# The last four tiles finished by VectorE alone, and an order of instructions searched at build

## The chip, the cores and the metric

The kernel runs on one NeuronCore of a Trainium2 chip. The metric is the device time of one execution in microseconds. It is given as the median of three runs. The core has a matrix engine (TensorE, PE in the profile, with its weight loads as PEld), three engines for elementwise work (VectorE or DVE, ScalarE or ACT, GpSimd or POOL), and SyncE (SP), whose queue issues nearly all the DMAs here.

## The reference

The input x has 4 rows of 1024 tokens with 512 features; each row has a condition vector of 256 numbers, which is used twice.

```python
hidden  = concatenate([cond, cond], axis=-1)                 # (4, 512)
x_mean  = mean(x, axis=1)                                    # (4, 1, 512)
fused   = concatenate([x, x_mean * ones, hidden * ones], -1) # (4, 1024, 1536)
out     = x + relu(einsum('bld,do->blo', fused, W) + b)      # W is (1536, 512)
```

The mean and the condition are the same for all tokens of a row. So the kernel computes, per row, one bias vector of 512 numbers from them, and multiplies only x with the first 512 rows of W. Everything is fp32.

## The kernel before, in words

The output is cut into 32 tiles of 128 tokens by 512 features, eight to a row. A tile is accumulated in one PSUM bank; five banks serve the tiles in turn (`O_BANKS`). [...] 

The stages around them are these.

- x comes in twice. For row 0 it is transposed on TensorE (`turn`, L299, pieces 0 to 9). For rows 1 to 3 it comes in again as `z`, in blocks of 32 tokens, and VectorE transposes it (L301, pieces 10 to 33). A piece is one slice `j` of a unit of one to four tiles.
- ScalarE rounds each piece to its high part and sums it over the tokens (`hi`, L318). VectorE, or POOL for some pieces of rows 1 and 2, subtracts to get the low part (`lo`, L334).
- Row r's sums go into `total`, and VectorE adds four products of W with them to an accumulator in PSUM (`term`, L396). The accumulator is split in two (`acc_hi`, `acc_lo`), and TensorE multiplies both with a constant matrix so that the bias stands in all 128 partitions (`bias_product`, L421). ScalarE copies it to SBUF (`bias`, L427).
- A finished tile goes through four steps. VectorE adds the bias while it moves the tile from PSUM to SBUF (`freed`, L505), which also frees the PSUM bank. ScalarE applies relu (L510), POOL adds x (`finished`, L513), and SP stores the tile (L525). The first four tiles are moved by ScalarE (L502) before the bias is there, and POOL adds it later. Tile 30 gets relu and x in one VectorE instruction (L518). Tile 31 is computed in two halves of 256 features. Each half gets the bias on TensorE, by two more matmuls (L484), and relu and x by L518.

The order of instructions on each engine is made at build by the class `Plan`. Each step is added with a key, the engines that can do it with a cost in microseconds, the keys that it depends on, a due time, and a function that emits it. Going backwards from the due times, `latest_starts` gives each step its latest start. `run` then repeatedly takes, among the steps that could start first on an engine, the one with the earliest latest start. `NEVER` is a due time that presses on nothing. The engines then execute their lists in order, waiting on semaphores. SP's queue keeps its order too: a store that waits for its tile holds the stores and loads behind it.

Of the kernel before, what the change touches and what calls it, by code (L numbers as in the profile page):

```python
# [1 line left out]

# [10 lines left out]
ALU = mybir.AluOpType  # L13
# [5 lines left out]
class Plan:  # L19
# [5 lines left out]


    HANDOVER = 0.2
    PATIENCE = 0.1

    def __init__(self, engines):  # L30
# [29 lines left out]
                        ready.append(d)  # L60
        return start

    def run(self):
        latest = self.latest_starts()
        assert len(latest) == len(self.todo)
        while self.todo:
            could = []
            for key, (costs, deps, _, _, _) in self.todo.items():
                if not all(d in self.done for d in deps):
                    continue  # L70
                options = []
                for engine, cost in costs.items():
                    start = self.free[engine]
                    for d in deps:
                        end, later, by = self.done[d]
                        if by != engine:
                            end += later + self.HANDOVER
                        start = max(start, end)
                    options.append((start + cost, start, engine, cost))
                _, start, engine, cost = min(options)  # L80
                could.append((start, latest[key], key, engine, cost))
            assert could, list(self.todo.items())[:8]
            first = min(could, key=lambda t: t[:2])
            start, _, key, engine, cost = min(
                (t for t in could if t[3] == first[3] and t[0] <= first[0] + self.PATIENCE),
                key=lambda t: (t[1], t[0]),
            )
            _, _, _, emit, later = self.todo.pop(key)
            self.log.append((start, engine, key, start - self.free[engine]))
            self.free[engine] = start + cost  # L90
            self.done[key] = (start + cost, later, engine)
            emit(engine)


@with_exitstack
def kernel(
# [23 lines left out]
    B, L, D = x.shape  # L120
# [14 lines left out]
    FIRST = 7.3  # L135
    NEVER = 1000.0
    TURN_PE = (0, 1, 2, 3)
    SINGLY = 2
    KEEP = 4
    LO_POOL = {(r, u, j) for r in (1, 2) for u in (0, 1) for j in (1, 3)}  # L140
# [113 lines left out]
    for n, u in enumerate(by_z):  # L254
        for i in range(NQ):
            deps = [("turn", c) for c in range(len(pieces)) if n >= Z_BUFS and pieces[c][0] == by_z[n - Z_BUFS]]
            plan.add(("z", u, i), {"sp": SPZ}, deps, NEVER,
                     lambda e, u=u, i=i: load_z(u, i), later=3.0)
    x_order = ["w", 0, 1, "cond"] + list(range(2, B * NK // G))
    for n, g in list(enumerate(x_order))[4:]:  # L260
        was = x_order[n - X_BUFS]
        deps = ([("w_lo", j) for j in range(J)] if was == "w" else
                [("add_cond", k) for k in range(KH)] if was == "cond" else
                [("finished", was * G + i) for i in range(G)])
        plan.add(("x", g), {"sp": 4 * SP}, deps, NEVER,
                 lambda e, g=g: load_x(g), later=3.0)

# [70 lines left out]
    for c, (u, js) in enumerate(pieces):  # L338
        r, k0, n = units[u]
        deps = ([x_here(t) for t in range(last_tile[u] - n + 1, last_tile[u] + 1)]  # L340
                if u in TURN_PE else [("z", u, i) for i in range(NQ)])
        if c:
            deps.append(("turn", c - 1))
        same = [v for v in range(c) if (v in by_pool) == (c in by_pool)]
        if len(same) >= 2:
            deps.append(("lo", same[-2]))
            if len(pieces[same[-2]][1]) > 1:
                deps.append(("sum", same[-2]))
        if r == 1 and c == first_piece[1]:
            deps.append(("term", 0, KH + J - 1))  # L350
        w = n * len(js)
        plan.add(("turn", c), {"pe": 0.12 * w} if u in TURN_PE else {"dve": 0.14 + 0.24 * w}, deps,
                 FIRST + 1.3 * c - 1.0 if u in TURN_PE else NEVER,
                 lambda e, c=c: turn(c))
        deps = [("turn", c)]
        if c >= S_BUFS:
            v, js_v = pieces[c - S_BUFS]
            deps += made(last_tile[v], js_v[-1])
        plan.add(("hi", c), {"act": 0.16 + 0.2 * (len(js) == 1) + 0.108 * w}, deps, NEVER,
                 lambda e, c=c: split_hi(c))  # L360
        plan.add(("lo", c), {"pool": 1.33} if c in by_pool else {"dve": 0.15 + 0.135 * w},
                 [("hi", c)], NEVER, lambda e, c=c: split_lo(e, c))
        if len(js) > 1:
            plan.add(("sum", c), {"dve": 0.65}, [("lo", c)], NEVER, lambda e, c=c: add_up(c))
# [105 lines left out]
    def product(t, j, h=None, parts=(0, 1, 2)):  # L470
        r, k = divmod(t, NK)
        u = unit_of[r, k]
        p = piece_of[u, j]
        c = pieces[p][1].index(j) * units[u][2] + k - units[u][1]
        c = slice(c * P, (c + 1) * P)
        key = t if h is None else (t, h)
        d = slice(0, D) if h is None else slice(h * D // 2, (h + 1) * D // 2)
        w = d.stop - d.start
        if key not in pos:
            todo[key] = 3 * J  # L480
            pos[key] = ps_o.tile([P, D], F32, tag="po", name=f"po{t}_{h}")
            if h is not None:
                for n, v in enumerate((acc_hi[r], acc_lo[r])):
                    nc.tensor.matmul(  # L484
                        pos[key][:, :w], lhsT=mean, rhs=v[:, d], start=(n == 0), stop=False
                    )
        for n in parts:
            v, m = ((hi, w_hi), (hi, w_lo), (lo, w_hi))[n]
            nc.tensor.matmul(  # L489
                pos[key][:, :w], lhsT=v[p][:, c], rhs=m[:, j, d],  # L490
                start=(h is None and todo[key] == 3 * J),
                stop=(todo[key] == 1),
            )
            todo[key] -= 1
# [6 lines left out]
    def keep(t):  # L501
        nc.scalar.activation(o_tile(t), pos[t], AF.Copy)  # L502

    def add_bias(e, t):
        nc_of[e].tensor_tensor(  # L505
            o_tile(t), outs[t] if t < KEEP else pos[t], biases[t // NK], ALU.add
        )

    def relu(t):
# [4 lines left out]

    def relu_add_x(t, h=None):
        d = slice(0, D) if h is None else slice(h * D // 2, (h + 1) * D // 2)
        v = outs[t] if h is None else pos[t, h][:, : D // 2]
        nc.vector.scalar_tensor_tensor(  # L518
            o_tile(t)[:, d], v, 0.0, x_tile(t)[:, d], ALU.max, ALU.add
        )  # L520
# [6 lines left out]
    for t in range(NT):  # L527
        r, k = divmod(t, NK)
        u = unit_of[r, k]
        for h in (0, 1) if t == LAST else (None,):  # L530
# [3 lines left out]
                free.append(("freed", t - O_BANKS))  # L534
            if h == 1:
                free.append(("freed", t + 1 - O_BANKS))
            if h == 0:
                free.append(("acc_lo", r))
            for j in range(J):
                c = piece_of[u, j]  # L540
# [15 lines left out]
                plan.add(("product", key, j), {"pe": 0.7 if h is None else 0.36},  # L556
                         deps, FIRST + 2.8 * t + (0.7 if h is None else 0.36) * (j + 1) + 1.4 * (h or 0), lambda e, t=t, j=j, h=h: product(t, j, h))
        room = [("stored", t - O_BUFS)] if t >= O_BUFS else []
        if t == LAST:
            for h in (0, 1):  # L560
                deps = [("product", (t, h) if h else t, J - 1), x_here(t)] + ([] if h else room)
                plan.add(("finish", t, h), {"dve": 0.42}, deps, NEVER, lambda e, t=t, h=h: relu_add_x(t, h))
                plan.add(("stored", t, h), {"sp": SP}, [("finish", t, h)], FIRST + 2.8 * t + 8,
                         lambda e, t=t, h=h: store(t, h), later=2.0)
            continue
        whole = made(t, J - 1)
        if t < KEEP:
            plan.add(("freed", t), {"act": 0.6}, whole, NEVER, lambda e, t=t: keep(t))
            plan.add(("added", t), {"pool": 1.33}, [("freed", t), ("bias", r)], NEVER, lambda e, t=t: add_bias(e, t))
            plan.add(("relu", t), {"act": 0.63}, [("added", t)], NEVER, lambda e, t=t: relu(t))  # L570
            biased = ("relu", t)
        else:
            plan.add(("freed", t), {"dve": 0.7}, whole + [("bias", r)] + room, NEVER,
                     lambda e, t=t: add_bias(e, t))
            biased = ("freed", t)
            if t < NT - 2:
                plan.add(("relu", t), {"act": 0.63}, [("freed", t)], NEVER, lambda e, t=t: relu(t))
                biased = ("relu", t)
        if t < NT - 2:
            plan.add(("finished", t), {"pool": 1.33}, [biased, x_here(t)], NEVER,  # L580
                     lambda e, t=t: add_x(t))
        else:
            plan.add(("finished", t), {"dve": 0.74}, [biased, x_here(t)], NEVER,
                     lambda e, t=t: relu_add_x(t))
        plan.add(("stored", t), {"sp": SP}, [("finished", t)], min(FIRST + 2.8 * (t + 9), FIRST + 2.8 * NT + 3), lambda e, t=t: store(t), later=2.0)

    plan.run()
    return plan
# [27 lines left out]
```

## Time and profile before

| what | value |
|---|---|
| median of 3 runs | 109.43 us (109.39 to 109.77) |
| the profiled execution, its own time | 110.05 us |
| span in its profile | 108.3 us |
| TensorE clock granted | 0.989 over the span |
| TensorE busy | 102.4 us, 95% |
| VectorE, ScalarE, POOL busy | 78.2, 56.0, 67.4 us |
| DMA moved | 26.31 MB |

The profile is of one execution, and the span runs from its first to its last instruction. The profiled execution took 1.8 us more than its span. Busy shares are averages over the whole span. Which engine sets the time is read from the chain that ended last: it goes back from the last instruction, at each step to what released it. Matmuls are pipelined, so a matmul row lasts about 0.40 us while the next one starts 0.23 us later; starts tell more than lengths.

### The profile page before, as it was taken

The page shows a single profiled execution, that of the slowest core. Times are in us where ns is not written, and L with a number is a line of the kernel's source. Part 1 is how long each engine was busy: PE and PEld are TensorE (multiplying, and loading weights), DVE is VectorE, ACT ScalarE, POOL GpSimd, SP SyncE. Part 2 cuts the span into 40 slices and gives each one's busy share as a digit, 9 for nine tenths or more (in the row PEclk, how much of TensorE's full clock was granted, in tenths as well). Part 3 has the DMA queues.
Part 4 walks back from the last instruction along what each step waited for, and adds up shares of the span by engine and source line. Part 5 has one row for each costly group of instructions (what it writes and reads, how often), then busy time and mean ns, then how long its engine had stood idle before and what let it go on. Part 6 is the DMA issues. An engine that isn't in the chain of part 4 may idle for free.

```text
span 108.3 us, 1476 instructions
## 1 busy us (share of the span) xinstructions
PE 102.4 (95%) x455; PEld 81.0 (75%) x455; DVE 78.2 (72%) x115; ACT 56.0 (52%) x126; POOL 67.4 (62%) x61
## 2 busy tenths in 40 slices
PE   5999999999999999999999999999999999999930
PEld 2466888887888878777887878878788787887920
DVE  1048932559999999839999999499999990462830
ACT  5047376798778794149657243295356040392000
POOL 5000009849999999999899996029640840099800
PEclk9999999999999999999999999999999999999995
DMA  3699999999999999999999999999983222015364
GB/s 92 180 368 397 379 432 203 197 201 200 202 203 193 265 208 227 282 250 279 332 398 355 286 338 285 259 400 403 397 322 123 97 97 97 0 41 223 124 232 156
DMA packets 22945, 26.31 MB, mean 243 GB/s; under 512 B 1173, under 2 KB 13721, under 8 KB 22810
## 3 DMA queue, kind: packets, MB, share of 16 engines
q1 hardware_dynamic: 22928, 26.22, 86.3%
q8 instruction: 3, 0.05, 0.2%
q14 instruction: 4, 0.03, 0.1%
q10 hardware_dynamic: 10, 0.01, 0.0%
HBM read 17.83 MB, written 8.39 MB: 242 GB/s over the span
## 4 chain that ended last, share of the span: by engine, by line
PE 94%; DVE 1%; ACT 1%; issue 0%
PE po_None L489 80%; PE xT L299 4%; PE pw L175 4%; PE po L489 3%; PE pb L421 2%; PE pw L308 1%; ACT hi L318 1%; PE po L484 0%; DVE o L518 0%; DVE warm L166 0%; PE pt L377 0%; DVE ones L168 0%
## 5 line engine op out<-in xcount | busy, mean ns | idle before, releaser
L489 PE MATMUL po_None<-w_hi,hi 128*128 128x512 f32 x124 | 49.7, 401 | 0.2 <-ACT hi L318 0.2
L513 POOL TENSOR_TENSOR o<-o,x 128x512 f32<-128x512 f32 x30 | 38.1, 1300 | 18.0 <-ACT o L510 16.1
L489 PE MATMUL po_None<-w_hi,lo 128*128 128x512 f32 x124 | 49.1, 397 | 0.0
L489 PE MATMUL po_None<-w_lo,hi 128*128 128x512 f32 x124 | 48.6, 396 | 0.0
L318 ACT ACTIVATE hi<-xT 128x512 fp32r<-128x512 f32 (+1 forms) x34 | 19.7, 579 | 20.7 <-DVE xT L301 11.4
L489 PEld LDWEIGHTS po_None<-w_hi,hi 128*128 128x128 f32 x124 | 23.4, 189 | 6.3 <-ACT hi L318 0.7
L489 PEld LDWEIGHTS po_None<-w_hi,lo 128*128 128x128 f32 x124 | 23.3, 188 | 5.5
L489 PEld LDWEIGHTS po_None<-w_lo,hi 128*128 128x128 f32 x124 | 23.3, 188 | 5.3
L301 DVE STREAM_TRANSPOSE xT<-z 128x512 f32<-128x512 f32 x24 | 25.5, 1102 | 0.2
L505 DVE TENSOR_TENSOR o<-po_None,bias 128x512 f32<-128x512 f32 x27 | 17.4, 684 | 11.2 <-issue 4.4
L334 DVE TENSOR_TENSOR lo<-xT,hi 128x512 fp32r<-128x512 f32 (+1 forms) x26 | 16.4, 640 | 11.9 <-ACT hi L318 11.7
L510 ACT ACTIVATE o<-o 128x512 f32<-128x512 f32 x30 | 17.9, 627 | 4.5 <-POOL o L505 2.4
L396 DVE SCALAR_TENSOR_TENSOR acc<-w_mean,tot,acc 128x512 f32<-128x512 f32 x16 | 12.1, 756 | 0.6
L385 POOL TENSOR_TENSOR wc<-w_cond 128x512 f32<-128x512 f32 x2 | 2.5, 1288 | 14.0 <-DMA w_cond<-in_L_cond_W_dram 14.0
L334 POOL TENSOR_TENSOR lo<-xT,hi 128x512 fp32r<-128x512 f32 x8 | 10.5, 1317 | 0.4 <-ACT hi L318 0.4
L427 ACT ACTIVATE bias<-pb 128x512 f32<-128x512 f32 x4 | 2.4, 599 | 11.3 <-PE pb L421 11.3
L299 PEld LDWEIGHTS xT<-ident,x 128*128 128x128 f32 x32 | 5.7, 206 | 1.3 <-issue 0.5
L318 ACT ACTIVATION_READ_ACCUMULATOR hi<-xT 128x1 f32 x32 | 6.2, 193 | 0.0
L407 POOL TENSOR_TENSOR cond<-cond,term 128x512 f32<-128x512 f32 x4 | 5.2, 1300 | 1.4 <-ACT term L402 1.2
L299 PE MATMUL xT<-ident,x 128*128 128x128 f32 x32 | 5.8, 298 | 0.0
L402 ACT ACTIVATE term<-wc,cT 128x512 f32<-128x512 f32 x8 | 5.5, 720 | 0.3 <-POOL cond L407 0.3
L407 POOL TENSOR_TENSOR cond<-bL,term 128x512 f32<-128x512 f32 x4 | 5.2, 1296 | 0.7 <-ACT term L402 0.7
(47 smaller groups left out, 54.6 us busy)
## 6 DMA issues: line engine op xcount, KB each, us to landing
out_dram<-o SPq DMA_DIRECT2D x31, 256.0 KB, 6.7
x<-in_x_dram SPq DMA_DIRECT2D x7, 1024.0 KB, 9.6
z<-in_x_dram SPq DMA_DIRECT2D x24, 256.0 KB, 9.7
w_x<-in_L_cond_W_dram SPq DMA_DIRECT2D x4, 256.0 KB, 6.0
w_cond<-in_L_cond_W_dram SPq DMA_DIRECT2D x1, 1024.0 KB, 9.8
w_mean<-in_L_cond_W_dram SPq DMA_DIRECT2D x1, 1024.0 KB
x<-in_x_dram SPq DMA_DIRECT2D x2, 256.0 KB, 3.6
x<-in_x_dram SPq DMA_DIRECT2D x1, 512.0 KB, 7.1
```

Source lines behind the costliest of these rows:

```text
L175: nc.tensor.matmul(pw, lhsT=warm[:, :P], rhs=warm, start=True, stop=True)
L299: nc.tensor.transpose(v[:, (m * n + i) * P : (m * n + i + 1) * P], x_t[:, j], ident)
L301: nc.vector.transpose(v[:, : n * P].rearrange("p (n t) -> p n t", t=Q), zs[u].rearrange("p n (a j) -> p n j a", j=J)[:, : n * NQ, js[0], :],)
L318: nc.scalar.activation(hi[c][:, :m], xT[c][:, :m], AF.Copy, accum_out=sums[:, r, js[0], s : s + 1] if len(js) == 1 else None,)
L334: nc_of[e].tensor_tensor(lo[c][:, :m], xT[c][:, :m], hi[c][:, :m].bitcast(F32), ALU.subtract)
L396: nc.vector.scalar_tensor_tensor(acc[r], w_mean[:, j, :], totals[r][:, j : j + 1], acc[r], ALU.mult, ALU.add)
L402: nc.scalar.activation(terms[r, k], wc[:, k], AF.Copy, scale=cT[:, k, r : r + 1])
L407: nc.gpsimd.tensor_tensor(conds[r], conds[r] if k else bL, terms[r, k], ALU.add)
L489: nc.tensor.matmul(pos[key][:, :w], lhsT=v[p][:, c], rhs=m[:, j, d], start=(h is None and todo[key] == 3 * J), stop=(todo[key] == 1),)
L505: nc_of[e].tensor_tensor(o_tile(t), outs[t] if t < KEEP else pos[t], biases[t // NK], ALU.add)
L510: nc.scalar.activation(outs[t], outs[t], AF.Relu)
L513: nc.gpsimd.tensor_tensor(outs[t], outs[t], x_tile(t), ALU.add)
```

## The change

The change has four parts.

1. The last four tiles (`ALONE = 28`) take neither ScalarE nor POOL. VectorE adds the bias in place in PSUM (`biased`), and a second VectorE instruction applies relu, adds x and writes the tile to SBUF. The left half of tile 31 gets its bias in this way too; the right half keeps the two bias matmuls.
2. The order is no longer the first that the rule gives. `simulate` runs the rule without emitting anything. `run` does this 1500 times, with some of the latest starts shifted by random amounts (a fixed seed), and keeps the order with the smallest sum of two simulated ends: the plain one, and one in which every engine but TensorE is 3% slower (`slower_end`).
3. New dependencies keep the order of buffers that rotate: z loads one after another, x loads one after another, `hi` and `freed` in order of pieces and tiles.
4. Due times of stores change: for a tile t, the smaller of its old rule and a fixed time near the end, and `NEVER` for the last four.

```diff
+    TRIES = 1500
+    SLOWER = 1.03
...
+        for n in range(self.TRIES):
+            trial = dict(shifts)
+            if best:
+                for key in luck.sample(list(latest), 1 + n % 12):
+                    trial[key] = luck.gauss(0.0, 3.0)
+            found = self.simulate({k: v + trial.get(k, 0.0) for k, v in latest.items()})
+            found = (found[1] + self.slower_end(found[0]),) + found
+            if not best or found[0] <= best[0]:
+                best, shifts = found, trial
+        _, self.log, _, self.free = best
+        for _, engine, key, _ in self.log:
+            self.todo[key][3](engine)
...
+    ALONE = 28
...
+            if n or i:
+                deps.append(("z", u, i - 1) if i else ("z", by_z[n - 1], NQ - 1))
...
+        if n > 4:
+            deps.append(("x", x_order[n - 1]))
...
-        deps = [("turn", c)]
+        deps = [("turn", c)] + ([("hi", c - 1)] if c else [])
...
-            if h is not None:
+            if h:
                 for n, v in enumerate((acc_hi[r], acc_lo[r])):
                     nc.tensor.matmul(
                         pos[key][:, :w], lhsT=mean, rhs=v[:, d], start=(n == 0), stop=False
...
+    def add_bias(e, t, h=None):
+        d = slice(0, D) if h is None else slice(h * D // 2, (h + 1) * D // 2)
+        v = outs[t] if t < KEEP else pos[t if h is None else (t, h)][:, : d.stop - d.start]
         nc_of[e].tensor_tensor(
+            v if t >= ALONE else o_tile(t), v, biases[t // NK][:, d], ALU.add
         )
...
-        v = outs[t] if h is None else pos[t, h][:, : D // 2]
+        v = pos[t] if h is None else pos[t, h][:, : D // 2]
...
+        if t:
+            room.append(("freed", t - 1))
+        due = min(FIRST + 2.8 * (t + 9), FIRST + 2.8 * NT - 8)
+        if t >= ALONE:
+            for h in (0, 1) if t == LAST else (None,):
+                key = (t, h) if h else t
+                cost = 0.7 if h is None else 0.42
+                ready = [("product", key, J - 1)]
+                if not h:
+                    plan.add(("biased", t), {"dve": cost}, ready + [("bias", r)], NEVER, lambda e, t=t, h=h: add_bias(e, t, h))
+                    ready = [("biased", t)] + room
+                plan.add(("freed", key), {"dve": cost}, ready + [x_here(t)], FIRST + 2.8 * (t + 1) + 1.5 + (h or 0),
+                         lambda e, t=t, h=h: relu_add_x(t, h))
+                plan.add(("stored", key), {"sp": SP}, [("freed", key)], NEVER,
                          lambda e, t=t, h=h: store(t, h), later=2.0)
             continue
```

The order that comes out differs from the old one as follows. SP's last stores were those of tiles 27, 30, 28, 29, 31 left, 31 right; they are now 24, 28, 25, 27, 29, 26, 30, 31 left, 31 right. POOL's last addition was tile 29; it is now tile 26, after 24, 25 and 27. The bias product of row 1 stood after the second slice of tile 12 and now stands before its first; that of row 2 stood after the first slice of tile 20 and now stands before the last slice of tile 19; that of row 3 stays after the first slice of tile 28. In the head TensorE takes the same single matmuls and transposes in another order. The x load of tiles 8 to 11 is issued in the middle of the `z` loads of unit 6 instead of after them, and that of tiles 16 to 19 after the store of tile 11 instead of before that of tile 8.

More of the change, by code (lines that the diff above doesn't have):

```diff
@@ L1 @@
+import random
 from contextlib import ExitStack
@@ L61, in latest_starts, with simulate @@
         return start
[L63 to L66, printed above, removed]
-            could = []
[L68 to L80, printed above, removed]
+    def simulate(self, latest):
+        free, done = dict(self.free), dict(self.done)
+        missing, followers, ready = {}, {}, []
+        for key, (_, deps, _, _, _) in self.todo.items():
+            open_deps = {d for d in deps if d not in done}
+            missing[key] = len(open_deps)
+            for d in open_deps:
+                followers.setdefault(d, []).append(key)
+            if not open_deps:
+                ready.append(key)
+        since = {}
+        log = []
+        while ready:
+            could = []
+            for key in ready:
+                costs, deps, _, _, _ = self.todo[key]
+                if key not in since:
+                    since[key] = {
+                        engine: max([0.0] + [
+                            end + (later + self.HANDOVER if by != engine else 0.0)
+                            for end, later, by in (done[d] for d in deps)
+                        ]) for engine in costs
+                    }
+                _, start, engine, cost = min(
+                    (max(free[e], since[key][e]) + c, max(free[e], since[key][e]), e, c)
+                    for e, c in costs.items()
+                )
                 could.append((start, latest[key], key, engine, cost))
-            assert could, list(self.todo.items())[:8]
             first = min(could, key=lambda t: t[:2])
@@ L87, in run, with slower_end @@
             )
[L88 to L92, printed above, removed]
+            ready.remove(key)
+            log.append((start, engine, key, start - free[engine]))
+            free[engine] = start + cost
+            done[key] = (start + cost, self.todo[key][4], engine)
+            for f in followers.get(key, ()):
+                missing[f] -= 1
+                if not missing[f]:
+                    ready.append(f)
+        assert len(log) == len(self.todo)
+        return log, max(free.values()), free
+    def slower_end(self, log):
+        free, done = dict(self.free), dict(self.done)
+        for _, engine, key, _ in log:
+            costs, deps, _, _, later = self.todo[key]
+            start = max([free[engine]] + [
+                end + (wait + self.HANDOVER if by != engine else 0.0)
+                for end, wait, by in (done[d] for d in deps)
+            ])
+            free[engine] = start + costs[engine] * (1.0 if engine == "pe" else self.SLOWER)
+            done[key] = (free[engine], later, engine)
+        return max(free.values())
+    def run(self):
+        latest = self.latest_starts()
+        luck = random.Random(1)
+        best, shifts = None, {}
+        for n in range(self.TRIES):
[10 more added lines that the diff above has]
+            self.todo[key][3](engine)
 @with_exitstack
@@ L490, in product @@
                 pos[key][:, :w], lhsT=v[p][:, c], rhs=m[:, j, d],
-                start=(h is None and todo[key] == 3 * J),
+                start=(not h and todo[key] == 3 * J),
                 stop=(todo[key] == 1),
@@ L502, in keep @@
         nc.scalar.activation(o_tile(t), pos[t], AF.Copy)
-    def add_bias(e, t):
+    def add_bias(e, t, h=None):
+        d = slice(0, D) if h is None else slice(h * D // 2, (h + 1) * D // 2)
+        v = outs[t] if t < KEEP else pos[t if h is None else (t, h)][:, : d.stop - d.start]
         nc_of[e].tensor_tensor(
-            o_tile(t), outs[t] if t < KEEP else pos[t], biases[t // NK], ALU.add
+            v if t >= ALONE else o_tile(t), v, biases[t // NK][:, d], ALU.add
         )
@@ L536 @@
                 free.append(("freed", t + 1 - O_BANKS))
-            if h == 0:
+            if h:
                 free.append(("acc_lo", r))
@@ L558 @@
         room = [("stored", t - O_BUFS)] if t >= O_BUFS else []
[L559 to L563, printed above, removed]
+        if t:
[12 more added lines that the diff above has]
+                plan.add(("stored", key), {"sp": SP}, [("freed", key)], NEVER,
                          lambda e, t=t, h=h: store(t, h), later=2.0)
             continue
-        whole = made(t, J - 1)
+        whole = made(t, J - 1) + ([("freed", t - 1)] if t else [])
         if t < KEEP:
@@ L569 @@
             plan.add(("added", t), {"pool": 1.33}, [("freed", t), ("bias", r)], NEVER, lambda e, t=t: add_bias(e, t))
-            plan.add(("relu", t), {"act": 0.63}, [("added", t)], NEVER, lambda e, t=t: relu(t))
-            biased = ("relu", t)
+            biased = ("added", t)
         else:
@@ L575 @@
             biased = ("freed", t)
[L576 to L585, printed above, removed]
+        plan.add(("relu", t), {"act": 0.63}, [biased], NEVER, lambda e, t=t: relu(t))
+        plan.add(("finished", t), {"pool": 1.33}, [("relu", t), x_here(t)], NEVER, lambda e, t=t: add_x(t))
+        plan.add(("stored", t), {"sp": SP}, [("finished", t)], due, lambda e, t=t: store(t), later=2.0)
     plan.run()
```

## The prediction

> **What bounds the kernel now.** I read the page first (busy shares), then the chain that ended last in order of time, then the timelines of VectorE (DVE), GpSimd (POOL) and SyncE (SP) over the last microseconds, then the DMA landings of two short windows. The page says which engine is full:
>
> ```profile
> span 108.3 us, 1476 instructions
> PE 102.4 (95%) x455; PEld 81.0 (75%) x455; DVE 78.2 (72%) x115; ACT 56.0 (52%) x126; POOL 67.4 (62%) x61
> PEclk9999999999999999999999999999999999999995
> ```
>
> The chain is TensorE from the head to the tail. Pieces of it (start, length in us, what):
>
> ```profile
> 48.92 20.56 PE po_None L489 x87
> ...
> 69.95 22.39 PE po_None L489 x96
> ...
> 100.50 0.23 PE po L484 x2
> 100.73 1.42 PE po L489 x12
> 102.16 0.24 PE po L484 x2
> 102.40 1.43 PE po L489 x12
> ...
> 103.85 0.42 DVE o L518
> ```
>
> From 8.54 on TensorE never stands still for more than 0.02 us, and a 512-wide matmul leaves every 0.233 us (20.56 / 87 is 0.236, 22.39 / 96 is 0.233) at the full clock. So no reordering can speed up the middle: it can only lose. Time can come from fewer matmuls and from what follows the last one. The span goes on to 108.26, that is 4.0 us after the last VectorE instruction ends at 104.27. What fills them (timelines of VectorE, POOL and SP):
>
> ```profile
> 101.32 1.73 DVE L518 SCALAR_TENSOR_TENSOR o<-o,x 128x512 f32<-128x512 f32 x1
> ```
> ```profile
> 101.22 1.28 POOL L513 TENSOR_TENSOR o<-o,x 128x512 f32<-128x512 f32 x1
> ```
> ```profile
> 103.50 0.38 SPq L525 DMA_DIRECT2D out_dram<-o  x1
> 103.98 0.40 SPq L525 DMA_DIRECT2D out_dram<-o  x1
> 104.47 0.40 SPq L525 DMA_DIRECT2D out_dram<-o  x1
> 104.97 0.52 SPq L525 DMA_DIRECT2D out_dram<-o  x1
> ```
>
> In program order SP issues the stores of tiles 27, 30, 28, 29, 31 left half, 31 right half. Tile 30's store is in front of those of 28 and 29, which POOL had finished at 101.26 and 102.50. It had to wait for VectorE's 1.73 us instruction (until 103.05) and went at 103.08. The other four followed about 0.49 us apart, so the last left at 104.97, 0.70 us after its data existed (104.27). The SP waits agree; the last row is the end of the kernel waiting for that store:
>
> ```profile
> SPq L525 <- DVE o L518: 3.0, 1, 3.0
> ...
> SPq L612 <- DMA out_dram<-o: 1.7, 1, 1.7
> ```
>
> The last store landed 2.28 us after its issue (107.25), and from there to 108.26 it is 1.0 us of closing steps.
>
> **The change, part by part.**
>
> *Fewer matmuls.* The left half of tile 31 no longer gets its bias through the two L484 matmuls, but from VectorE. Removed: 2 x 256-wide, the 0.23 us row at 100.50. It is on the chain: -0.23. The right half keeps its two (the 0.24 row). The last matmul ends at 103.58.
>
> *VectorE's tail.* Tiles 28 to 30: bias added in place in PSUM (nearest row L505, 0.68 us), then relu and x from PSUM. For the second the trace has a SCALAR_TENSOR_TENSOR 512 wide with one PSUM and one SBUF tensor input, the L396 row, 0.756 us. A pair is 1.45 us, against 2.8 us of matmuls per tile, so it stays hidden until tile 30: matmuls end 100.50, bias 100.59 to 101.28, relu and x 101.3 to 102.05. Left half of 31: matmuls end 101.93, two 256-wide instructions of 0.42 (L518 row) end at 102.85. Right half: 103.58 + 0.04, 0.42 long, ends at 104.04. Before it was 104.27. ScalarE and POOL lose tiles 28 and 29 (0.63 and 1.3 us each), which no end waits for.
>
> The 1.73 us row asks whether the new pairs will be stretched too. The old tile-30 instruction read o and x, both in SBUF, while POOL's add read SBUF, and ended 0.55 us after POOL's (102.50). [...] I take 0.75. [...]
>
> *SP.* The new order is 24, 28, 25, 27, 29, 26, 30, 31 left, 31 right. POOL's last add is now tile 26: four adds from 94.97 in the order 24, 25, 27, 26 end at 100.02. The last four stores then go at about 100.05, 102.07, 102.88 and 104.07: SP is idle before each. The last leaves at 104.07 and not 104.97: -0.90, of which 0.23 is the matmuls' share and 0.67 the queue's. Landing:
>
> ```profile
> out_dram<-o SPq DMA_DIRECT2D x4, 256.0 KB, 2.0
> ```
> ```profile
> out_dram<-o SPq DMA_DIRECT2D x2, 128.0 KB, 2.3
> ```
>
> The first row is the window from 96 to 100.9 us (stores that go alone), the second the window from 103 (1 MB in five stores within 2 us, DMA near 400 GB/s). Alone, 128 KB should not take longer than 256 KB: 2.0 instead of 2.28, -0.28. [...] Rows first: I take between 2.0 and 2.3, nearer to 2.0: -0.2. Both ends go into the range.
>
> *The head.* The same transposes and parts in another order. Counted from 8.54 at 0.233 each: the fourth slice of W (w_hi ready 10.04) is wanted at 10.51 instead of 12.85, the third at 10.04 (ready 9.53), w_lo of the fourth at 11.84 (VectorE makes it by about 10.8). lo of pieces 2 and 3 come 0.6 us before their buffers are wanted. Slack is small but positive, and the number of instructions is equal: 0.
>
> *Row handovers.* These are the tightest waits of before: tile 13 started 0.05 us after its PSUM bank was freed (bias of row 1: matmuls 46.87, copy 47.54, add 48.17 to 48.86), tile 21 0.57 us, tile 29 0.51 us. The new order puts row 1's bias product two products (1.4 us) and row 2's one product (0.7 us) earlier and leaves row 3's. Walking row 1 on VectorE by its rows: hi of row 0 is whole about 1 us earlier (transposes 8 and 9 stand earlier), so the four L396 terms of row 0 end near 25.9; then four transposes (1.0 each), lo and freed as listed, total of row 1 at 38.3, terms to 41.6, freed 7, lo 16, acc_lo of row 1 at 43.5, lo 14 at 44.1. TensorE wants acc_lo at 45.4 and lo 14 at 45.9: 1.8 us to spare. Row 2's transposes 28 to 33 now stand behind freed 20 (72.7): lo 28 at 75.4 for 81.7, acc_lo of row 3 at 88.1 for 92.2. POOL's adds are permuted within rows at 1.25 us each: lo 17 comes at 45.0 (wanted 48.0).
>
> *Loads.* x for tiles 16 to 19 is now issued behind the store of tile 11, near 58.9 instead of 52.08. With the 11 us that this load took it lands near 70, about when the relu of tile 16 is ready (70.6). Only POOL's adds wait for it, and behind those only stores. x for the last four tiles goes out near 74 instead of 69.4, wanted at 96.6. Cover is large: 0. The ten o buffers: freed 10 (51.3) wants store 0, issued near 38.7 and landed by 48.
>
> **Sum.** -0.23 - 0.67 - 0.2 = -1.1 us. The profiled execution (span 108.26, 110.05 with what lies around it) goes to a span of 107.15 and about 108.95; the median of the runs shown, 0.6 lower than the profiled one, from 109.43 to 108.3.
>
> **The rivals.**
> *Only the matmuls arrive.* A store stays queued before the last one: if POOL's last add (26) comes 3 us late, stores 26, 30 and both halves go in one burst as before. Then 0.23 is left and 109.2 follows, no change that can be told (a measurement of this kernel separates about 0.5%, 0.55 us). For it: 26 stands in front of 30 in a queue that keeps order. Against it: POOL starts at 94.97 with nothing before 24. 10%.
>
> *A stall in the middle.* Row 1's bias product is now in front of product 12, and lo 14 is the last of its group on VectorE. If acc_lo of row 1 is ready at 45.4 + d, TensorE loses d, and never gets it back, since it is full from there on. It decides from 1.9 us later than my walk; the gain is used up at 3.0, and 3.6 late gives over 110.0. VectorE was 99% busy from 30 to 40 us, so delays add up: a late z load (the x load of tiles 8 to 11 now goes ahead of half of z 6) or a POOL lo that holds a transpose would do it. The head's fourth W slice (0.47 us of slack) is a smaller copy of this. Against it: each step of the walk has a row. 110.2, 12%.
>
> **How the numbers follow.** The forecast, 108.3, has 78%; its own range is 108.0 (landing 2.0, no loss) to 108.7 (landing 2.3 and a small head stall). With the first rival's part and the noise of the three runs (0.38 us) the range is 107.9 to 109.0. Faster 0.78, same 0.10, slower 0.12.
>
> **What would show it.** Right: L484 x2 fewer matmuls and a chain without stalls to about 103.6; last VectorE instruction ending near 104.05; no 1.73 us instruction; last store issued within 0.1 us of it; end of span 3.1 to 3.3 us after the issue. Wrong: a wait of PE on DVE or ACT of over 0.3 us near 10, 45 or 48 us; stores issued 0.49 us apart at the end; the span's end more than 3.3 us behind the last issue.

## The result, and the profile after

Six runs of the changed kernel have a median of 108.1 us (107.53 to 108.65), six of the kernel before 109.6 us (109.39 to 110.08). The ratio is 0.9862 with a 95% interval of 0.9824 to 0.9900: about 1.5 us less, between 1.1 and 1.9. The profiled execution took 108.65 us with a span of 106.9 us, 1.4 us under that of before.

The page's first lines, and pieces of the chain that ended last (start, length in us, what):

```profile
span 106.9 us, 1459 instructions
PE 100.9 (94%) x453; PEld 80.2 (75%) x453; DVE 78.8 (74%) x118; ACT 55.1 (52%) x124; POOL 64.7 (61%) x59
```

```profile
1.63 5.72 DMA x<-in_x_dram
...
8.83 2.83 PE po_None L543 x11
...
46.42 21.69 PE po_None L543 x93
...
92.81 7.69 PE po_None L543 x33
100.50 1.43 PE po L543 x12
101.93 0.23 PE po L538 x2
102.17 1.43 PE po L543 x12
103.60 0.02 issue
103.62 0.42 DVE o L574
```

L543 issues the product matmuls, as L489 did before: twelve of 128x512 to a tile, that is w_hi with hi, w_lo with hi and w_hi with lo for each of four slices of 128 features (tile 31 has twelve of 128x256 to each half). The first L484 pair is gone: only one `x2` row of L538 is left. The chain still ends with VectorE's half of tile 31, at 104.05 instead of 104.27. At the front, tile 1's x load now stands in the chain with 5.72 us: in this execution it was late, and the third matmul of the products started at 8.83 instead of 8.54.

The end, on VectorE, on SP and in the DMA view of the window from 102 to 105 us:

```profile
100.54 0.70 DVE L561 TENSOR_TENSOR po_None<-po_None,bias 128x512 f32<-128x512 f32 x1 [1.38 <-PE po_None L543]
101.28 0.69 DVE L574 SCALAR_TENSOR_TENSOR o<-po_None,x 128x512 f32<-128x512 f32 x1
101.97 0.43 DVE L561 TENSOR_TENSOR po<-po,bias 128x256 f32<-128x256 f32 x1
102.50 0.43 DVE L574 SCALAR_TENSOR_TENSOR o<-po,x 128x256 f32<-128x256 f32 x1
103.62 0.42 DVE L574 SCALAR_TENSOR_TENSOR o<-po,x 128x256 f32<-128x256 f32 x1 [0.70 <-PE po L543]
```

```profile
101.99 0.33 SPq L581 DMA_DIRECT2D out_dram<-o  x1
102.95 0.33 SPq L581 DMA_DIRECT2D out_dram<-o  x1
104.07 0.33 SPq L581 DMA_DIRECT2D out_dram<-o  x1
```

```profile
out_dram<-o SPq DMA_DIRECT2D x1, 256.0 KB, 2.0
out_dram<-o SPq DMA_DIRECT2D x2, 128.0 KB, 1.7
```

The 1.73 us instruction is gone. Each store leaves right behind its data, the last one 0.02 us after VectorE instead of 0.70, and it lands sooner, in 1.75 us instead of 2.30 (here and below from its issue to the end of SP's wait for it, which comes 0.02 to 0.03 us after the landing itself).

The span can be cut at four points that every trace shows. The third matmul of the products is the first that follows both head loads (those of x's second tile and of W's first slice). From there TensorE is full in these two executions, but for the stall shown below. Where the products begin early, as in some runs further on, TensorE loses part of the lead again by 11 us: 0.34 us in e1 and 0.49 in e4, in both at the transposes of tiles 2 and 3.

| stretch of the span, us | before | after |
|---|---|---|
| start to the third product matmul | 8.54 | 8.83 |
| from there to the start of the last matmul | 94.99 | 94.47 |
| last matmul's start to last store's issue | 1.44 | 0.77 |
| issue to landing | 2.30 | 1.75 |
| landing to the end | 0.99 | 1.05 |
| sum | 108.26 | 106.86 |

The second row lost 0.52 us: 0.23 for the two matmuls, and 0.29 more. The tile-13 handover shows these. First the kernel before, then the changed one (TensorE's timeline, first column the start):

```profile
48.27 0.40 PE L489 MATMUL po_None<-w_lo,hi 128*128 128x512 f32 x1
48.50 0.40 PE L489 MATMUL po_None<-w_hi,lo 128*128 128x512 f32 x1
48.92 0.50 PE L489 MATMUL po_None<-w_hi,hi 128*128 128x512 f32 x1
49.25 0.39 PE L489 MATMUL po_None<-w_lo,hi 128*128 128x512 f32 x1
```

```profile
48.58 0.40 PE L543 MATMUL po_None<-w_lo,hi 128*128 128x512 f32 x1
48.81 0.40 PE L543 MATMUL po_None<-w_hi,lo 128*128 128x512 f32 x1
49.04 0.40 PE L543 MATMUL po_None<-w_hi,hi 128*128 128x512 f32 x1
```

Before, the starts are 0.42 and 0.34 us apart around 48.92, where 0.23 is the rule; that is 0.29 us lost. After, they are 0.23 apart. The chain that ended last had shown 0.02 us of it, since a matmul's row (0.40 us) is longer than its spacing (0.23).

### The profile page after: what moved, and what is told of

Its sections match the earlier page's. It is cut to its first block, busy times and chain, and to the rows that moved or that the text cites. A ratio compares the mean times of both kernels' runs of the same rounds, so it can differ in the third digit from the quotient of the medians.

```text
span 106.9 us, 1459 instructions
## 1 busy us (share of the span) xinstructions
PE 100.9 (94%) x453; PEld 80.2 (75%) x453; DVE 78.8 (74%) x118; ACT 55.1 (52%) x124; POOL 64.7 (61%) x59
## 4 chain that ended last, share of the span: by engine, by line
PE 89%; DMA 5%; SPq 1%; ACT 1%; DVE 0%; issue 0%
PE po_None L543 81%; DMA x<-in_x_dram 5%; PE xT L353 3%; PE po L543 3%; PE pb L475 2%; ACT hi L372 1%; DVE o L574 0%; SPq L282 0%; SPq L261 0%; PE po L538 0%; PE pt L431 0%
## 5 line engine op out<-in xcount | busy, mean ns | idle before, releaser
L543 PE MATMUL po_None<-w_hi,hi 128*128 128x512 f32 x124 | 49.3, 399 | 0.2 <-ACT hi L372 0.2
L543 PE MATMUL po_None<-w_hi,lo 128*128 128x512 f32 x124 | 48.7, 396 | 0.0
L543 PE MATMUL po_None<-w_lo,hi 128*128 128x512 f32 x124 | 48.7, 397 | 0.0
L569 POOL TENSOR_TENSOR o<-o,x 128x512 f32<-128x512 f32 x28 | 35.5, 1296 | 18.2 <-ACT o L566 18.2
L543 PEld LDWEIGHTS po_None<-w_hi,hi 128*128 128x128 f32 x124 | 23.3, 188 | 6.1 <-ACT hi L372 0.7
L543 PEld LDWEIGHTS po_None<-w_hi,lo 128*128 128x128 f32 x124 | 23.3, 188 | 5.4
L543 PEld LDWEIGHTS po_None<-w_lo,hi 128*128 128x128 f32 x124 | 23.3, 188 | 5.4
L561 DVE TENSOR_TENSOR o<-po_None,bias 128x512 f32<-128x512 f32 x24 | 15.4, 681 | 9.2 <-issue 4.9
L566 ACT ACTIVATE o<-o 128x512 f32<-128x512 f32 x28 | 17.0, 630 | 5.3 <-DVE o L561 2.5
L353 PEld LDWEIGHTS xT<-ident,x 128*128 128x128 f32 x32 | 4.9, 206 | 2.2 <-DMA x<-in_x_dram 1.8
L353 PE MATMUL xT<-ident,x 128*128 128x128 f32 x32 | 5.0, 285 | 1.3 <-DMA x<-in_x_dram 1.3
L465 ACT ACTIVATE acc_hi<-acc 128x512 fp32r<-128x512 f32 x4 | 2.4, 594 | 6.0 <-DVE acc L450 6.0
```

What stands on the lines that cost most here:

```text
L353: nc.tensor.transpose(v[:, (m * n + i) * P : (m * n + i + 1) * P], x_t[:, j], ident)
L543: nc.tensor.matmul(pos[key][:, :w], lhsT=v[p][:, c], rhs=m[:, j, d], start=(not h and todo[key] == 3 * J), stop=(todo[key] == 1),)
L561: nc_of[e].tensor_tensor(v if t >= ALONE else o_tile(t), v, biases[t // NK][:, d], ALU.add)
L566: nc.scalar.activation(outs[t], outs[t], AF.Relu)
L569: nc.gpsimd.tensor_tensor(outs[t], outs[t], x_tile(t), ALU.add)
```

## The experiments

Two theories stood against each other. A: the gain is a sum of a few places, namely two matmuls, the stall at tile 13, the store queue and the landing. B: it comes from the searched order as a whole, or from relieving POOL and ScalarE. The stretches of the table above tell them apart better than the times, because the start of the products varied from 7.57 to 8.83 us between profiled executions of kernels with the same first loads in the same order (8.83 and 8.27 in two executions of the changed kernel itself).

**The stores alone (e1).** The kernel before with one move in the list of emitted steps:

```diff
+        self.move(("stored", 30), ("stored", 31, 0))   # behind those of 28 and 29
```

> The kernel before, with one edit: SyncE issues tile 30's store after those of tiles 28 and 29. Theory A (the end was held by SP's queue): the stores of 28 and 29 leave by 102.6 us, tile 30's at 103.08, the halves at 103.5 and about 104.3; the last leaves 0.05 us after its data instead of 0.70, so the span loses about 0.65 us by the issue, and some 0.1 to 0.4 us more because the last store meets less traffic. Time about 108.6 where the kernel before has 109.6. Rival B (the gain of the change came from its whole order and the matmuls, the DMA engines being full at the end anyway): the last store leaves earlier but lands at the same time, span within 0.2 us of before.

Measured: 108.45 us, 109.98 for the kernel before on the same chip, ratio 0.9868 (0.9829 to 0.9907). From the last matmul to the last issue 0.77 us instead of 1.44, landing 1.74 instead of 2.30: 1.23 us by these two. The rest of the 1.5 us between the times is in the head: in the profiled execution the products began 0.73 us earlier than in that of before, and the second stretch, with the stall at tile 13 still in it, was 0.38 us longer (95.37). VectorE and SP of this kernel:

```profile
100.97 1.73 DVE L527 SCALAR_TENSOR_TENSOR o<-o,x 128x512 f32<-128x512 f32 x1
```

```profile
103.95 0.33 SPq L534 DMA_DIRECT2D out_dram<-o  x1
```

The long instruction is still there, and costs nothing here, with no finished tile queued behind it. One moved store brings most of what the change gains behind the head: 1.23 us, where the change has 0.52 + 0.67 + 0.55 = 1.74. B's form (DMA engines full anyway) falls.

**The long instruction alone (e12).** The kernel before with its stores in their old order, but tile 30 kept in PSUM:

```diff
-            o_tile(t), outs[t] if t < KEEP else pos[t], biases[t // NK], ALU.add
+            pos[t] if t == NT - 2 else o_tile(t), outs[t] if t < KEEP else pos[t], biases[t // NK], ALU.add
...
-        v = outs[t] if h is None else pos[t, h][:, : D // 2]
+        v = pos[t] if h is None else pos[t, h][:, : D // 2]
```

> The kernel before in its own order, stores included, with one edit: tile 30's bias stays in place in PSUM, and its second VectorE instruction reads PSUM and one SBUF tensor instead of two SBUF tensors. Theory A (the store queue was late because this instruction waited for POOL's last addition): it lasts 0.69 us instead of 1.73, tile 30's store leaves 1.0 us earlier, those of 28 and 29 and the halves follow, the last within 0.1 us of its data, 0.65 us earlier than before; landing between 1.75 and 2.0 instead of 2.30: -0.9 to -1.2 us, 108.6 where the kernel before has 109.7. Rival B (the stores of 28 and 29 hold the queue however early tile 30's leaves): last issue still 0.4 us or more behind its data, no more than -0.3 us.

Measured: 108.65 us, 110.05 for the kernel before, ratio 0.9880 (0.9857 to 0.9903). Its VectorE row, and POOL beside it:

```profile
100.83 0.69 DVE L518 SCALAR_TENSOR_TENSOR o<-po_None,x 128x512 f32<-128x512 f32 x1
```

```profile
100.72 1.28 POOL L513 TENSOR_TENSOR o<-o,x 128x512 f32<-128x512 f32 x1
```

Beside the same POOL addition the instruction took 0.69 us with one input from PSUM, and 1.73 in the kernel before with both from SBUF. The last store's issue is again 0.77 us behind the last matmul. Its landing is 1.94: its neighbours still leave in a row (101.55, 101.97, 102.44, 102.94, 103.79), so more stores are under way with it than in e1; that this lengthens the landing fits all three kernels (2.30 in the kernel before, 1.94 here, 1.74 in e1), but was not tested alone. Queue order and instruction were two ends of one delay; mending either is enough for the issue.

**The handover alone (e2).** The kernel before, and row 1's bias product ahead of tile 12:

```diff
+        self.move(("bias_product", 1), ("product", 12, 0))
```

> The kernel before, with one edit: row 1's bias product stands before tile 12's first slice instead of after its second. Theory A: the first matmul of tile 13 follows the one ahead of it after 0.23 us and not 0.42, and the next after 0.23 and not 0.34, so 0.29 us less from there to the last matmul; nothing else moves: -0.3 us, 109.3 where the kernel before has 109.6. Rival B: the 0.42 and 0.34 us are how the trace models the ends of matmuls and not lost time, or the wait moves to tile 12; then the last matmul comes as late as before, 0.0 us.

Measured: 109.5 us, 109.98 for the kernel before, ratio 0.9962 (0.9935 to 0.9989). The second stretch is 94.68 us instead of 94.99, -0.31, and the matmuls at tile 13 start 0.23 apart:

```profile
48.34 0.40 PE L498 MATMUL po_None<-w_lo,hi 128*128 128x512 f32 x1
48.57 0.40 PE L498 MATMUL po_None<-w_hi,lo 128*128 128x512 f32 x1
48.80 0.40 PE L498 MATMUL po_None<-w_hi,hi 128*128 128x512 f32 x1
49.03 0.40 PE L498 MATMUL po_None<-w_lo,hi 128*128 128x512 f32 x1
```

The stall was lost time and not the trace's model.

**The handover undone (e6).** The changed kernel with the bias product back behind tile 12's second slice:

```diff
+        self.move(("product", 12, 0), ("bias_product", 1))
+        self.move(("product", 12, 1), ("bias_product", 1))
```

> The changed kernel in its own order, with one edit: row 1's bias product goes back behind tile 12's second slice. Theory A: the stall at tile 13 comes back, 0.42 and 0.34 us between matmuls that else follow at 0.23, so +0.29 us from the third product matmul to the last: 108.4. Rival B: VectorE's other order (freed 8 before transposes 20 and 21 anyway) has the bank free in time, 0.0.

Measured: second stretch 94.76 us, +0.29 on the changed kernel's 94.47, with the 0.42 and 0.34 us starts back at tile 13. The time, 108.56 us (ratio to the kernel before 0.9854, 0.9809 to 0.9899), cannot tell that from none by itself.

**Two matmuls put back (e3).** The changed kernel's order; the left half of tile 31 takes its bias from TensorE, and VectorE's step for it is empty:

```diff
-            if h:
+            if h is not None:
...
-                start=(not h and todo[key] == 3 * J),
+                start=(h is None and todo[key] == 3 * J),
...
-    lambda e, t=t, h=h: add_bias(e, t, h))
+    lambda e, t=t, h=h: add_bias(e, t, h) if h is None else None)
```

> The changed kernel in its own order, with one edit: the left half of tile 31 gets its bias from two 256-wide matmuls again, and VectorE's bias addition for it is left out. Theory A: the last matmul starts 0.23 us later measured from the third matmul of the products, everything behind it shifts by the same, and the end is otherwise that of the changed kernel (last store within 0.1 us of its data, landing 1.75): +0.23 us, 108.3 where the changed kernel has 108.1. Rival B (TensorE's end is covered by VectorE's pairs): 0.0.

Measured: second stretch 94.73 us, +0.26; the rest as in the changed kernel (0.77 to the issue, 1.74 to the landing). The pair is back in the chain:

```profile
99.68 0.23 PE po L538 x2
99.92 1.42 PE po L543 x12
101.34 0.24 PE po L538 x2
```

The time, 108.12 us (ratio 0.9848, 0.9814 to 0.9882), does not show 0.23 us; the trace does.

**The first order instead of the best of 1500 (e4).** `TRIES = 1`, everything else as changed.

> The changed kernel with one try of the search instead of 1500: all its new steps, dependencies and due times, but the first order that the rule gives, in which row 1's bias product stands after tile 12's second slice again. Theory A: the end keeps its gain (last store within 0.1 us of its data), and only the stall at tile 13 comes back, 0.2 to 0.3 us: 108.4 where the changed kernel has 108.1. Rival B (the search carries the gain): the larger part of 1.5 us comes back, 109.2 or more.

Measured: 108.32 us, ratio 0.9854 (0.9816 to 0.9893). Issue 0.77 behind the last matmul, landing 1.74. The stall at tile 13 is back. The wait of 0.49 us before the first transposes of tiles 2 and 3 also shows: the products began early (7.57) and caught up with that load. The second stretch is 95.31. The search is not what carries the gain.

**By hand on the kernel before (e7).** Bias product moved, stores in the order 28, 30, 29 and halves, tile 30 in PSUM, left half of 31 with VectorE's bias. Tiles 28 and 29 stay with ScalarE and POOL, and there is no search:

```diff
+        self.move(("stored", 28), ("stored", 30))
+        self.move(("bias_product", 1), ("product", 12, 0))
...
+        if h == 0:
+            nc.vector.tensor_tensor(v, v, biases[t // NK][:, d], ALU.add)
```

> The kernel before with four edits by hand and no search: row 1's bias product before tile 12; stores in the order 28, 30, 29, halves; tile 30's bias in place in PSUM; the left half of tile 31 gets its bias from VectorE and loses its two bias matmuls. Tiles 28 and 29 stay with ScalarE and POOL. Theory A (the gain is the sum of few places): last matmul -0.23 -0.29, last store within 0.1 us of its data, landing under 2.0 us: span 1.4 to 1.7 us under the kernel before, that is the time of the changed kernel, about 108.0 where the kernel before has 109.6. Rival B (the searched order or the relief of POOL and ScalarE is needed): no more than half of it, 108.8 or more.

Measured: 108.03 us, 109.98 for the kernel before, ratio 0.9833 (0.9797 to 0.9868). Second stretch 94.64 (with 0.11 us waited for the load of tiles 2 and 3), 0.77 to the issue, 1.73 to the landing. The end of its chain:

```profile
101.16 0.23 PE po L494 x2
101.40 1.43 PE po L499 x12
102.83 0.02 issue
102.85 0.42 DVE o L530
```

Four edits give what the change gives. The relief of POOL and ScalarE and the search are not needed for it.

**In place, or not (e9).** The changed kernel's order, with the bias of tiles 28 to 30 and of the left half added into SBUF:

```diff
-            v if t >= ALONE else o_tile(t), v, biases[t // NK][:, d], ALU.add
+            o_tile(t)[:, d], v, biases[t // NK][:, d], ALU.add
...
-        v = pos[t] if h is None else pos[t, h][:, : D // 2]
+        v = outs[t][:, d] if not h else pos[t, h][:, : D // 2]
```

> The changed kernel in its own order, with one edit: the bias of the last four tiles is added into the SBUF output tile instead of in place in PSUM, and the second VectorE instruction reads two SBUF tensors. Theory A (two SBUF inputs and POOL's additions exclude each other, but only the last two stores set the end): the second instructions of tiles 28 and 29, which fall into POOL's four additions (95.0 to 100.0 us), last 1.0 to 1.7 us instead of 0.69; those of 30 and 31 fall behind them and keep 0.69 and 0.42; the end does not move: 0.0 us, 108.1. Rival B (in place is what frees the end): tile 30 or 31 is stretched too and the last store goes 0.5 us or more later, 108.6 or more.

```profile
95.73 1.42 DVE L574 SCALAR_TENSOR_TENSOR o<-o,x 128x512 f32<-128x512 f32 x1
97.07 0.68 DVE L561 TENSOR_TENSOR o<-po_None,bias 128x512 f32<-128x512 f32 x1
97.78 1.07 DVE L574 SCALAR_TENSOR_TENSOR o<-o,x 128x512 f32<-128x512 f32 x1
...
100.34 0.69 DVE L574 SCALAR_TENSOR_TENSOR o<-o,x 128x512 f32<-128x512 f32 x1
```

POOL's four additions, first in this kernel, then in the changed one:

```profile
94.04 5.96 POOL L569 TENSOR_TENSOR o<-o,x 128x512 f32<-128x512 f32 x4 [5.54 <-ACT o L566]
```

```profile
94.97 5.05 POOL L569 TENSOR_TENSOR o<-o,x 128x512 f32<-128x512 f32 x4 [5.54 <-ACT o L566]
```

Tiles 28 and 29 are stretched to 1.42 and 1.07 us, POOL's four additions from 5.05 us to 5.96, and tile 30, behind them, is not. The end stays (0.77, 1.73), the time is 107.83 us (ratio 0.9816, 0.9782 to 0.9850). The second stretch is 94.73, 0.26 us longer, and 0.17 of it stands in two wider starts near 9.5 us, again after an early begin of the products (7.64). "In place in PSUM" is worth nothing in this order: POOL is done at 100.00, before the second instruction of tile 30 begins at 100.34.

**Another cut of tile 31 (e8).** `CUT = 384` in place of 256.

> The changed kernel with one edit: tile 31 is cut into 384 and 128 features instead of 256 and 256. Theory A (a matmul's spacing goes with its width, 0.233 us for 512): the last matmul starts when it did, VectorE's last instruction has 128 columns and lasts about 0.29 us instead of 0.42, the last store has 64 KB instead of 128 and lands 0.1 us sooner: -0.2 us, 107.9. Rival B (a 128-wide matmul cannot follow in less than about the 0.117 us that the transposes of 128 columns take): 14 of them cost 0.8 us more, the left part 0.7 us more and nothing is saved by it: +0.6 us, 108.7.

The matmuls of 128 columns started 0.112 us apart, against 0.118 for 256 columns and 0.175 for 384. So 12 x 0.175 + 14 x 0.112 is 3.67 us where 26 x 0.118 is 3.07: by this the last matmul comes 0.6 us later. The second stretch was 1.02 us longer (95.49); the other 0.4 us stand in four starts near 8.6 to 10.3 us that are 0.33 to 0.34 us apart, which the cut of tile 31 does not touch. VectorE's last instruction took 0.29 us, and the landing of 64 KB 1.61. The time was 108.32 us (ratio 0.9853, 0.9821 to 0.9886), no better. Rival B's spacing held, and its 0.6 us is what the cut costs TensorE; but it had the saving at nothing, and from the last matmul to the issue it was 0.63 us instead of 0.77.

**The head (e11, e14, with e13 beside it).** The second x tile was late in the changed kernel's profile, so its load went ahead of W's first slice:

```diff
-        (("w", 0), 4.1, lambda: load_w(0)),
         (("x", 0, 1), 4.2, lambda: load_x(0, 1, 1)),
+        (("w", 0), 4.1, lambda: load_w(0)),
```

> The changed kernel with one edit in the head: SyncE issues the load of x's second tile before that of W's first slice instead of after it. Seen so far: the second tile's transposes started anywhere from 6.2 to 7.4 us in the profiled executions, and the third product matmul from 7.6 to 8.8, while everything behind it takes the same time. Theory A (the second tile's load sets the start): it lands about 0.7 us earlier, the third product matmul starts near 8.0 at the latest: -0.3 us against the changed kernel, 107.8. Rival B (W's first slice is wanted as urgently, and now comes later by as much): no gain, 108.1, or a loss of up to 0.4 us.

It gave 107.98 us with a ratio of 0.9810 (0.9786 to 0.9833), which looked like a gain on the changed kernel's 0.9862. So both were run again, on the same chip.

> The changed kernel again, unedited, beside the next one on the same chip. Expected 108.1 us, third product matmul between 7.6 and 8.8 us, 94.5 us from there to the last matmul's start, last store's landing 1.74 us.

> The changed kernel with the load of x's second tile before that of W's first slice, again, beside the unedited one. Theory A (the head gains): 0.2 to 0.5 us under the unedited one. Rival B (the two loads only change places in what is waited for): within 0.15 us of it; then the lower ratio seen in the last call came from the draw of the heads.

Measured: 107.94 us for the unedited kernel (ratio 0.9849, 0.9811 to 0.9888) and 107.95 for the edited one (0.9866, 0.9817 to 0.9915). In e11 the wait had moved to W's first slice (ScalarE 0.36 us idle for it). No gain shows, though the intervals leave room for a few tenths of a microsecond either way. The second stretch was 94.47 in both, the same as in the changed kernel's first profile.

## Why the prediction was right, point by point

- *Matmuls*: -0.23 forecast; -0.23 as chain rows here, +0.26 with the pair put back.
- *VectorE's tail*: forecast to end at 104.04, measured 104.05. The agreement is partly luck: the head started 0.29 us late, and the stall that I had not counted gave 0.29 us back. The same pair of errors keeps the times of POOL and SP below near their forecast. That the PSUM pairs would not be stretched was my estimate from the L396 row. They took 0.69 to 0.70 us per instruction and not the 0.756 of L396, also those of tiles 28 and 29 (95.94 to 99.17), which ran beside POOL's four additions (94.97 to 100.02).
- *SP*: the last four stores forecast at 100.05, 102.07, 102.88 and 104.07; measured 100.05, 101.99, 102.95 and 104.07. The queue's share, -0.67, is measured at -0.67 by e1, by e12 and by the change. That the old instruction was long because both inputs came from SBUF beside a POOL addition is shown by e12 (same addition, one input in PSUM: 0.69 us) and e9 (both inputs in SBUF, POOL idle: 0.69; POOL busy: 1.42 and 1.07). Tile 30 met no POOL addition in the new order: POOL was done at 100.02, as in my sum, and tile 30's first instruction began at 100.54.
- *Landing*: mis-sized. I took -0.2 from between 2.0 and 2.3; it was -0.55. The lone 256 KB store (2.0) was an upper bound, not the price of 128 KB, which landed in 1.73 to 1.75 us as the last store of the changed kernel, e1, e3, e4, e7 and e9. For 64 KB it was 1.61 (e8).
- *Handovers*: the term "0" failed. I read from the chain that TensorE "never stands still for more than 0.02 us" and that reordering "can only lose". A line of my own on the handovers (tile 13 started 0.05 us after its PSUM bank was freed) said that it had waited. It was 0.29 us, and the moved bias product took it away. The walk itself held: acc_lo of row 1 forecast for 43.5 and lo 14 for 44.1, measured at 43.52 and 44.12; freed 20 at 72.9 (72.7), lo 28 at 75.5 (75.4), acc_lo of row 3 at 88.0 (88.1).
- *Head*: "0" is right for the work, but the start of the products differs between executions (7.57 to 8.83 us), by more than several of the terms; what sets it was not found. I had given the noise by the three runs' spread (0.38 us), which was too small.
- *Rivals*: POOL's last addition ended at 100.02 as assumed, so no store was queued; no stall came at row 1 (its bias product started 2.26 us after acc_lo was ready).

So the sum -1.1 missed two terms of one sign, -0.35 of the landing and -0.29 of the stall, and the profiled execution's late head (0.29) and longer close (0.06) hid part of them: -1.40 in its span. The median moved by about 1.5.

## What to carry to other kernels

At the end of a kernel look at the order of the last stores in their queue, not only at the last computation: here a store that waited for a 1.73 us instruction left at 103.08 and held two tiles finished at 101.26 and 102.50 behind it, and the last landing, behind the burst that followed, took 2.30 us where the changed kernel has 1.75. Find lost time on TensorE by the distance between matmul starts (here 0.42 and 0.34 us instead of 0.23), not by the idle time that the rows show (here 0.02). When a large edit gains a little over one per cent, cut the span at fixed events and put back one piece at a time; here one moved store was enough for most of the gain.

## What the runs showed of the hardware that was not expected

- The changed kernel's last store, 128 KB issued 1.12 us after the one before it, landed in 1.75 us, the 64 KB one of e8 in 1.61, and 256 KB stores that went alone (before, 96 to 100.9 us) in 2.0; the last 128 KB of the 1 MB that before issued from 103.08 to 104.97 needed 2.30.
- Where VectorE instructions with two SBUF inputs met POOL additions in e9, both sides were slower: the two instructions took 1.42 and 1.07 us instead of 0.69, and four POOL additions 5.96 instead of 5.05. Beside the 1.73 us instruction of the kernel before, POOL's addition kept its 1.28 us.
- Matmuls of 128 columns started 0.112 us apart in e8, those of 256 columns 0.118 in the kernel before: half the columns cost nearly the same. Narrower ones were not run.
- The second x tile's load landed at 7.35 us in the changed kernel's profile, and its transposes started at 7.39; in e3 and e7, with the same loads issued before it, they started at 6.83 and 6.73.
